# Token rows in a recommender kernel: every second gather adds its rows in the DMA, additions with a lag of three groups

## The chip, the cores and the metric

The kernel runs on one core of one Trainium2 chip. The metric is the device time of one launch in microseconds (us), as the median of several runs without a profile. The kernel before takes 5566.13 us (three runs, 5557.75 to 5580.29).

## What is computed

A batch of 16,384 samples goes through embedding lookups and a small MLP. The reference, cut to what matters:

```
tok = word_emb[token_idx].mean(axis=1)      # 32 rows of 300 floats from a table of 50,000
e1  = emb_mh1[mh1_idx].mean(axis=1)         # 20 rows of 64, likewise e2 and e3
o1  = emb_oh1[oh1_idx]                      # one row of 64, likewise o2 to o4
emb = concatenate([tok, e1, e2, e3, o1, o2, o3, o4], axis=1)      # 748 wide
wide = sums of one-column tables at the same indices
h = relu(emb @ W1 + b1); h = relu(h @ W2 + b2); h = relu(h @ W3 + b3)
return sigmoid(h @ Wd + bd + wide)
```

Only the first line is touched by the change: for each sample the sum of 32 rows of `word_emb`.

## The kernel before

The samples are cut into 128 tiles of 128, one sample on each partition, and four tiles make a block of 512. The main loop goes over the tiles, and inside a tile over `STEPS` = 11 steps. A step does a slice of three tiles' work, so that the engines overlap:

- `one_hots` (line 260): two VectorE (DVE) comparisons make one-hot rows for six pairs of samples of the current tile, one step ahead. Their inputs lie in SBUF.
- `counts` (line 278): 64-row matmuls on TensorE (PE) turn them into counts by table row. ScalarE (ACT) copies the counts from PSUM to FP8 (line 285).
- `tokens` (lines 180 to 206): the gathers of the token rows and their additions, of the current tile.
- `small_sums` (line 303): matmuls of the previous tile's counts with the small tables. DVE reduces the results into the tile `g` (line 310).
- `mlp` (`layer`, line 353): the MLP of the last complete block in float32 matmuls. ACT applies bias and ReLU (line 362).

The class `Paced` hands out the last three, as generators, in equal parts over the steps. Nothing reorders the instructions afterwards (`manual_schedule`): each engine executes its own in the order in which the loop writes them. When a block's four `g` tiles are complete, `transposed` (lines 345 and 346) turns them with PE and DVE into the MLP's input `x`. After the last tile there is one more iteration with only sums and MLP steps, and after it the last block's MLP runs alone.

The tokens: a tile of 128 samples needs 32 indirect DMAs, one for each index column. Each is issued by GpSimd (POOL) on line 188 and brings 128 rows of 300 floats, one to a partition. Four of them fill one buffer of the pool `tok`, which has three. A buffer's rows have a pitch of 320 floats and begin 32 floats into it. Three additions on DVE follow in program order, directly after a group's gathers: two rows with two rows (line 196, 600 elements), then one with one (line 204, 300 elements), then the sum into `g` (line 205); for a tile's first group the last two are one addition straight into `g` (line 202). There are eight groups a tile. The first gather of a group waits until DVE is done with the group three back, since that one held the same buffer. Every gather has one of eight DMA semaphores in turn, and waits for the gather eight back, which used it before.

Of the kernel before, what the change touches and what calls it, by code (L numbers as in the profile page):

```python
# [8 lines left out]
F32 = mybir.dt.float32  # L9
# [3 lines left out]
U32 = mybir.dt.uint32  # L13
AF = mybir.ActivationFunctionType
ALU = mybir.AluOpType
AX = mybir.AxisListType

P = 128
N_TOK, TOK_D = 32, 300
N_MH, EMB = 20, 64  # L20
ROW = EMB + 1
D1, D2, D3 = 1024, 512, 256
TOK_GROUP = 4
TOK_PITCH = 320
BLOCK = 512
HALF = P // 2
N_SMALL = 3 * N_MH + 4
# [1 line left out]
STEPS = -(-HALF // ONEHOT)  # L29
# [15 lines left out]
def kernel(  # L45
# [21 lines left out]
    nc = tc.nc  # L67
# [7 lines left out]
    for f in SMALL:  # L75
        n = -(-tables[f].shape[0] // P)
# [1 line left out]
        n_h += n  # L78
    PER_BANK = 512 // n_h

    tokp = ctx.enter_context(tc.tile_pool(name="tok", bufs=3))
    const = ctx.enter_context(tc.tile_pool(name="const", bufs=1))
    idxp = ctx.enter_context(tc.tile_pool(name="idx", bufs=2))
    keyp = ctx.enter_context(tc.tile_pool(name="keys", bufs=1))
# [40 lines left out]
    first = const.tile([P, 2, N_SMALL], I32, name="first")  # L125
# [10 lines left out]
    for part0 in range(0, n_h, PART):  # L136
        raw = cp.tile([P, PART, ROW], F32, name="raw", tag="counts")
        for f in SMALL:
            table, (h0, h1) = tables[f], slices[f]
            full, rest = divmod(table.shape[0], P)  # L140
            a, b = max(h0, part0), min(h0 + full, part0 + PART)
            if a < b:
                nc.sync.dma_start(
                    out=raw[:, a - part0 : b - part0, :],
                    in_=table[(a - h0) * P : (b - h0) * P, :].rearrange("(h p) d -> p h d", p=P),
# [4 lines left out]
        for a in range(0, PART, 23):  # L150
            b = min(a + 23, PART)
# [25 lines left out]
    bd_sb = const.tile([1, 1], F32, name="bd_sb")  # L177
    nc.scalar.dma_start(out=bd_sb, in_=bd)

    def tokens(g, it):  # L180

        for q in range(N_TOK // TOK_GROUP):

            space = tokp.tile([P, TOK_GROUP * TOK_PITCH + 64], F32, name="tok_rows")
            rows = space[:, 32 : 32 + TOK_GROUP * TOK_PITCH].rearrange("p (t d) -> p t d", d=TOK_PITCH)
            for t in range(TOK_GROUP):
                j = q * TOK_GROUP + t
                nc.gpsimd.indirect_dma_start(  # L188
                    out=rows[:, t, 0:TOK_D],
                    out_offset=None,  # L190
                    in_=word,
                    in_offset=bass.IndirectOffsetOnAxis(ap=it[:, j : j + 1], axis=0),
                )
            n = TOK_GROUP // 2
            while n > 1:
                nc.vector.tensor_add(  # L196
                    rows[:, 0:n, 0:TOK_D], rows[:, 0:n, 0:TOK_D], rows[:, n : 2 * n, 0:TOK_D]
                )
                n //= 2
            first, second = rows[:, 0, 0:TOK_D], rows[:, 1, 0:TOK_D]  # L200
            if q == 0:
                nc.vector.tensor_add(g[:, 0:TOK_D], first, second)
            else:
                nc.vector.tensor_add(first, first, second)  # L204
                nc.vector.tensor_add(g[:, 0:TOK_D], g[:, 0:TOK_D], first)  # L205
            yield 1

    def load_indices(blk):

# [202 lines left out]
    it, ix = load_indices(0)  # L412
# [3 lines left out]
    for t in range(tiles + 1):  # L416
        s = t % NSUB
        sums = None
        if before:
            sums = Paced(small_sums(*before), n_h + LULL, STEPS)  # L420
        if t < tiles:
            if s == 0 and t:
                it, sc = next_it, next_sc
            g = gp.tile([P, G_COLS], F32, name="g")
            cnt = cp.tile([P, 2, HALF, n_h], FP8, name="cnt", tag="counts")
            toks = Paced(tokens(g, it[:, s, :].bitcast(U32)), N_TOK // TOK_GROUP, STEPS)
        for i in range(STEPS):
# [12 lines left out]
            if sums:  # L440
                sums.go()
            if layers:
                layers.go()
        if before:
            sums.finish()
            gs.append(before[0])
            wides.append(wide_term(before[0]))
        before = (g, cnt) if t < tiles else None
        if len(gs) == NSUB:
            if layers:  # L450
                layers.finish()
            layers = Paced(mlp(t // NSUB - 1, transposed(gs), wides), mlp_size, NSUB * STEPS)
            gs, wides = [], []
# [40 lines left out]
```

## Time and profile before

| | us |
|---|---|
| median of three runs without a profile | 5566.13 |
| the profiled execution | 7340.1 |
| its span, first to last instruction | 7338.3 |
| POOL busy (4096 gathers of 0.997 us) | 4082.8 |
| PE busy, by the profile | 5808.1 |
| DVE busy | 3542.7 |
| ACT busy | 2657.3 |

The profiled execution is a third longer than the runs without a profile. An engine's busy time is the sum of its instructions' durations; ends of matmuls are modelled, so PE's is rough. In a group's line, `out<-in` are the program's tile names, followed by the number of instructions, their busy time in us, the mean ns of one, and the idle time of the engine just before them with what ended most of it. In a timeline each row has a start in us, a duration in us, the engine, the line, the operation, and in brackets the idle time before it with its releaser; `issue` means that the engine waited for nothing that the profile shows. The DMA queue `q0` is the one that POOL's gathers use; its share is that of 16 DMA engines over the span.

### The profile page before, as it was taken

How to read it: one execution, taken by the hardware profiler on the slowest of the kernel's cores; microseconds unless marked ns; L12 is line 12 of the kernel's file. 1: busy time of each engine (PE TensorE's matmuls, PEld its weight loads, DVE VectorE, ACT ScalarE, POOL GpSimd, SP SyncE). 2: the span in 40 equal slices, each digit the busy share in tenths (PEclk: the TensorE clock that was granted, in tenths of full speed). 3: DMA queues.
4: the chain of work that ended last, by engine and by line, in shares of the span. 5: the costliest groups of instructions: out<-in, count | busy, mean ns of one | idle time of the engine just before them, and what ended most of it. 6: DMA issues, size and time to landing. Idle time of an engine off the chain costs nothing.

```text
span 7338.3 us, 100239 instructions
## 1 busy us (share of the span) xinstructions
PE 5808.1 (79%) x40960; PEld 3442.6 (47%) x40960; DVE 3542.7 (48%) x6977; ACT 2657.3 (36%) x3383; POOL 4082.8 (56%) x4103
## 2 busy tenths in 40 slices
PE   2688888888778787888878788878877878888789
PEld 2444444444444444444444444444444444444444
DVE  4444445445444454445445445445544444445442
ACT  4333333333333333333333333333333333333332
POOL 5555555555555555555555555555555555555551
PEclk8798888888888888888899998888898989888899
DMA  4333333333333333333333333333333333333330
GB/s 130 94 89 92 88 89 90 91 90 88 88 90 89 88 85 90 89 88 90 93 89 94 90 90 89 91 86 91 88 89 90 88 87 90 93 89 88 86 91 25
DMA packets 242809, 652.34 MB, mean 89 GB/s; under 512 B 105631, under 2 KB 109471, under 8 KB 242347
## 3 DMA queue, kind: packets, MB, share of 16 engines
q0 software_dynamic: 196608, 629.41, 31.9%
q1 hardware_dynamic: 42738, 10.83, 0.8%
q8 instruction: 320, 5.24, 0.3%
q10 hardware_dynamic: 3001, 5.69, 0.2%
q14 instruction: 142, 1.16, 0.1%
HBM read 645.59 MB, written 0.07 MB: 88 GB/s over the span
## 4 chain that ended last, share of the span: by engine, by line
PE 59%; another core or an unknown queue 20%; ACT 10%; issue 7%; DVE 3%; DMA 0%; SPq 0%; DVEq 0%; ACTq 0%
PE ph L353 27%; PE pg L303 21%; PE pc L278 9%; ACT cnt L285 9%; PE pt L345 1%; ACT h L362 1%; DVE x L346 1%; DVE g L310 1%; PE po L375 1%; PE pk L243 0%; PE po L377 0%; DMA raw<-in_mh_dram 0%; DVE slice L260 0%; DVE tok_rows L196 0%
## 5 line engine op out<-in xcount | busy, mean ns | idle before, releaser
L188 POOL DMA_INDIRECT tok_rows<-in_word_emb_dram,it x4096 | 4081.9, 997 | 3120.9 <-DVE g L205 1202.3
L285 ACT ACTIVATE cnt<-pc 128x828 fp8e3<-128x828 f32 (+1 forms) x2816 | 2239.5, 840 | 3521.0 <-remote 1890.0
L303 PE MATMUL pg<-terms,cnt 128*128 128x195 bf16 x17664 | 2142.2, 271 | 372.5 <-issue 308.3
L260 DVE TENSOR_TENSOR row<-iota,sc 128x768 bf16<-128x768 bf16 (+1 forms) x1408 | 765.2, 543 | 2667.3 <-remote 1545.4
L303 PEld LDWEIGHTS <-cnt 128*128 128x128 fp8e3 x17664 | 1748.2, 147 | 629.6 <-issue 485.2
L353 PE MATMUL ph<-x,w_sb 128*128 128x512 f32 (+1 forms) x3072 | 1600.2, 647 | 27.1 <-issue 26.1
L278 PE MATMUL pc<-slice,row 64*128 64x138 bf16 x16384 | 858.3, 231 | 940.4 <-ACT cnt L285 640.7
L278 PEld LDWEIGHTS <-row 64*128 64x128 bf16 x16384 | 558.1, 97 | 2050.2 <-issue 1556.8
L353 PE MATMUL ph<-h,w_sb 128*128 128x512 f32 x2560 | 1341.1, 648 | 26.5 <-issue 24.6
L353 PEld LDWEIGHTS ph<-x,w_sb 128*128 128x128 f32 (+1 forms) x3072 | 579.6, 209 | 502.4 <-issue 489.1
L260 DVE TENSOR_TENSOR slice<-iota,sc 128x828 bf16<-128x828 bf16 (+1 forms) x1408 | 808.7, 574 | 0.0
L196 DVE TENSOR_TENSOR tok_rows<-tok_rows 128x600 f32<-128x600 f32 x1024 | 795.2, 777 | 1.0 <-DMA tok_rows<-in_word_emb_dram,it 0.7
L353 PEld LDWEIGHTS ph<-h,w_sb 128*128 128x128 f32 x2560 | 485.3, 210 | 415.5 <-issue 415.4
L362 ACT ACTIVATE h<-ph,b_sb 128x512 f32<-128x512 f32 x448 | 308.3, 688 | 948.6 <-PE ph L353 495.9
L310 DVE TENSOR_REDUCE g<-pg 128x130 f32<-128x390 f32 (+1 forms) x512 | 251.6, 510 | 787.3 <-remote 286.4
L204 DVE TENSOR_TENSOR tok_rows<-tok_rows 128x300 f32<-128x300 f32 x896 | 423.7, 473 | 30.8
L205 DVE TENSOR_TENSOR g<-g,tok_rows 128x300 f32<-128x300 f32 x896 | 422.0, 471 | 30.7
L346 DVE TENSOR_SCALAR x<-pt,scale 128x512 f32<-128x512 f32 (+1 forms) x192 | 139.6, 749 | 116.1 <-PE pt L345 74.9
L345 PE MATMUL pt<-ident,g 128*128 128x128 f32 (+1 forms) x768 | 132.3, 311 | 71.3 <-DVE x L346 70.3
L345 PEld LDWEIGHTS pt<-ident,g 128*128 128x128 f32 (+1 forms) x768 | 92.6, 154 | 110.0 <-DVE x L346 100.5
L243 PE MATMUL pk<-ident_bf,keys 128*128 128x128 bf16 x128 | 23.7, 241 | 86.7 <-DVE keys L238 85.0
L285 ACT ACT_TABLE_LOAD x31 | 39.8, 1283 | 143.2 <-PE pc L278 143.2
(35 smaller groups left out, 458.7 us busy)
## 6 DMA issues: line engine op xcount, KB each, us to landing
tok_rows<-in_word_emb_dram,it POOLq DMA_INDIRECT x4096
ix<-in_idx_dram SPq DMA_DIRECT2D x128, 32.0 KB
w_sb<-in_W_dram ACTq DMA_DIRECT2D x6, 512.0 KB
w_sb<-in_W_dram ACTq DMA_DIRECT2D x1, 2048.0 KB
it<-in_idx_dram SPq DMA_DIRECT2D x32, 64.0 KB
out_dram<-h SPq DMA_DIRECT2D x32, 2.0 KB
raw<-in_mh_dram SPq DMA_DIRECT2D x1, 422.5 KB
w_sb<-in_W_dram ACTq DMA_DIRECT2D x1, 256.0 KB
```

The costliest lines, as they stand in the source:

```text
L188: nc.gpsimd.indirect_dma_start(out=rows[:, t, 0:TOK_D], out_offset=None, in_=word, in_offset=bass.IndirectOffsetOnAxis(ap=it[:, j : j + 1] ...
L196: nc.vector.tensor_add(rows[:, 0:n, 0:TOK_D], rows[:, 0:n, 0:TOK_D], rows[:, n : 2 * n, 0:TOK_D])
L204: nc.vector.tensor_add(first, first, second)
L205: nc.vector.tensor_add(g[:, 0:TOK_D], g[:, 0:TOK_D], first)
L260: nc.vector.tensor_tensor(one[:, 0:rows, :].rearrange("p i (n d) -> p i n d", d=2), iota[:, 0:n].rearrange("p (n d) -> p n d", d=2).unsque ...
L278: nc.tensor.matmul(pc[:, f, k * n_h : (k + 1) * n_h], hot[0][half, k0 + k, :], hot[1][half, k0 + k, :], start=True, stop=True,)
L285: nc.scalar.activation(cnt[:, :, b + k0 : b + k0 + n, :].rearrange("l f k h -> l f (k h)"), pc[:, :, 0 : n * n_h], AF.Copy, scale=0.5, sat ...
L303: nc.tensor.matmul(pg[:, j, :], by_slice[:, :, h], terms[:, h, :], start=(h == h0), stop=(h == h1 - 1))
L310: nc.vector.tensor_reduce(g[:, at : at + n * ROW].rearrange("p (f d) -> p f d", f=n), pg[:, 0:n, :].rearrange("p f (c d) -> p f d c", c=3) ...
L345: nc.tensor.transpose(pt[:kk, s * P : (s + 1) * P], chunk(g, k), ident)
L353: nc.tensor.matmul(ph, weights[:kk, k, m * P : (m + 1) * P], src[:kk, k, :], start=(k == 0), stop=(k == len(kks) - 1),)
L362: nc.scalar.activation(dst[:, m, :], ph, AF.Relu, bias=bias[:, m : m + 1])
```

## The change

A group now has two row buffers, side by side without padding, and stands for four gathers: two plain ones that fill it, and two that add their rows to it in the DMA (`compute_op` add). Plain and adding gathers alternate: between the plain gathers of a group stand the adding gathers of the group before it. The order on POOL is: plain for group q, part 0; add for group q-1, part 0; plain for q, part 1; add for q-1, part 1. This runs on over the borders of tiles. An adding gather waits until the plain gather of the same part, five places before it on POOL, has landed. DVE's additions for a group come three groups later: the two halves into one (300 elements), and the sum into `g` (300 elements); for a tile's first group it is one addition into `g`. The pool `tok` has six buffers in place of three. So the last groups of a tile are added up during the next tile's first steps; `last_tokens` does what is left after the last tile, ahead of the final iteration's steps. The number of gathers stays 4096. Instructions on PE and ACT and their order are as before.

```diff
-TOK_GROUP = 4
-TOK_PITCH = 320
+TOK_GROUP = 2
+TOK_LAG = 3
...
-    tokp = ctx.enter_context(tc.tile_pool(name="tok", bufs=3))
+    tokp = ctx.enter_context(tc.tile_pool(name="tok", bufs=2 * TOK_LAG))
...
+    under_way = []
+
+    def gather(rows, t, it, j, op):
+        nc.gpsimd.indirect_dma_start(
+            out=rows[:, t * TOK_D : (t + 1) * TOK_D],
+            out_offset=None,
+            in_=word,
+            in_offset=bass.IndirectOffsetOnAxis(ap=it[:, j : j + 1], axis=0),
+            compute_op=op,
+        )
+
+    def add_up(rows, g, first):
+        a, b, n = rows[:, 0:TOK_D], rows[:, TOK_D : 2 * TOK_D], TOK_D
+        if first:
+            nc.vector.tensor_add(g[:, 0:n], a, b)
+        else:
+            nc.vector.tensor_add(a, a, b)
+            nc.vector.tensor_add(g[:, 0:n], g[:, 0:n], a)
+
     def tokens(g, it):
...
+        for q in range(N_TOK // (2 * TOK_GROUP)):
+            rows = tokp.tile([P, TOK_GROUP * TOK_D], F32, name="tok_rows")
             for t in range(TOK_GROUP):
...
+                gather(rows, t, it, q * 2 * TOK_GROUP + t, ALU.bypass)
+                if under_way:
+                    old, _, old_it, old_q = under_way[-1]
+                    gather(old, t, old_it, (old_q * 2 + 1) * TOK_GROUP + t, ALU.add)
+            under_way.append((rows, g, it, q))
+            if len(under_way) > TOK_LAG:
+                rows, to, _, old_q = under_way.pop(0)
+                add_up(rows, to, old_q == 0)
             yield 1
+
+    def last_tokens():
+        rows, _, it, q = under_way[-1]
+        for t in range(TOK_GROUP):
+            gather(rows, t, it, (q * 2 + 1) * TOK_GROUP + t, ALU.add)
+        for rows, g, _, q in under_way:
+            add_up(rows, g, q == 0)
...
-            toks = Paced(tokens(g, it[:, s, :].bitcast(U32)), N_TOK // TOK_GROUP, STEPS)
+            toks = Paced(tokens(g, it[:, s, :].bitcast(U32)), N_TOK // (2 * TOK_GROUP), STEPS)
+        else:
+            last_tokens()
```

More of the change, by code (lines that the diff above doesn't have):

```diff
@@ L180, in tokens @@
     def tokens(g, it):
-        for q in range(N_TOK // TOK_GROUP):
-            space = tokp.tile([P, TOK_GROUP * TOK_PITCH + 64], F32, name="tok_rows")
-            rows = space[:, 32 : 32 + TOK_GROUP * TOK_PITCH].rearrange("p (t d) -> p t d", d=TOK_PITCH)
+        for q in range(N_TOK // (2 * TOK_GROUP)):
+            rows = tokp.tile([P, TOK_GROUP * TOK_D], F32, name="tok_rows")
             for t in range(TOK_GROUP):
[L187 to L205, printed above, removed]
-            yield 1
```

## The prediction

> **What bounds the kernel now.** I read the page's busy shares first, then the costliest groups, then the waits of POOL, then the timeline of POOL and of PE.
>
> ```profile
> span 7338.3 us, 100239 instructions
> ...
> PE 5808.1 (79%) x40960; PEld 3442.6 (47%) x40960; DVE 3542.7 (48%) x6977; ACT 2657.3 (36%) x3383; POOL 4082.8 (56%) x4103
> ...
> q0 software_dynamic: 196608, 629.41, 31.9%
> ...
> L188 POOL DMA_INDIRECT tok_rows<-in_word_emb_dram,it x4096 | 4081.9, 997 | 3120.9 <-DVE g L205 1202.3
> ```
>
> By shares PE looks like the bound. But this profiled execution took 7340.1 us (span 7338.3) and the median without a profile is 5566.13, so PE's 5808 us of busy time cannot all be real: it is longer than the whole unprofiled run. The span holds stretches in which every engine stands still, and the unprofiled run has no room for them. So I ask what each engine needs when nothing holds it up.
>
> POOL first. Its timeline, in a stretch where it has buffers:
>
> ```profile
> 3003.55 0.95 POOL L188 DMA_INDIRECT tok_rows<-in_word_emb_dram,it  x1 [0.30 <-issue]
> 3004.81 0.95 POOL L188 DMA_INDIRECT tok_rows<-in_word_emb_dram,it  x1 [0.30 <-issue]
> 3012.30 0.94 POOL L188 DMA_INDIRECT tok_rows<-in_word_emb_dram,it  x1 [6.54 <-DVE g L205]
> ```
>
> A gather (128 rows of 300 floats) keeps POOL 0.95 us, and the next starts 0.30 us after it: 1.25 us from start to start. The mean is 0.997 us, so 4096 gathers need 4096 x (0.997 + 0.305) = 5333 us. The first starts at 38 us and the last ends at 7204, 134 us before the end (last additions, last sums, last MLP). 38 + 5333 + 134 = 5505 us: 61 us, 1.1%, under the unprofiled median. In the profile POOL idles besides (us in total, times, longest):
>
> ```profile
> POOL tok_rows L188 <- DVE g L205: 1202.3, 337, 10.0
> ...
> POOL tok_rows L188 <- DVE g L202: 753.6, 110, 16.4
> ```
>
> The 1956 us behind DVE are waits for a free row buffer, in steps that PE held up; they are the slack of the profiled execution (7338 - 5505 = 1833 us), and without the profile 61 us of it are left. POOL is the bound, at about 99%.
>
> PE next. In a dense stretch, one step of the main loop to the next:
>
> ```profile
> 7197.05 0.54 PE L278 MATMUL pc<-slice,row 64*128 64x138 bf16 x12
> ...
> 7200.54 0.54 PE L278 MATMUL pc<-slice,row 64*128 64x138 bf16 x12
> ```
>
> 3.49 us a step, 11 steps a tile are 38.4 us, and about 2 us of a tile are its share of a block's transposes and last layer (3022.1 to 3029.9 in the timeline, over four tiles): 40.4 us, against 32 x 1.302 = 41.7 us on POOL. PE is second by about 1.3 us a tile, 170 us in all. DVE needs 3542.7 / 128 = 27.7 us a tile and ACT 20.8.
>
> Last, DVE's additions, and what they do to POOL:
>
> ```profile
> L196 DVE TENSOR_TENSOR tok_rows<-tok_rows 128x600 f32<-128x600 f32 x1024 | 795.2, 777 | 1.0 <-DMA tok_rows<-in_word_emb_dram,it 0.7
> ...
> L204 DVE TENSOR_TENSOR tok_rows<-tok_rows 128x300 f32<-128x300 f32 x896 | 423.7, 473 | 30.8
> L205 DVE TENSOR_TENSOR g<-g,tok_rows 128x300 f32<-128x300 f32 x896 | 422.0, 471 | 30.7
> ```
>
> The timeline shows a gather beside them:
>
> ```profile
> 3015.78 0.78 DVE L196 TENSOR_TENSOR tok_rows<-tok_rows 128x600 f32<-128x600 f32 x1
> 3016.05 1.33 POOL L188 DMA_INDIRECT tok_rows<-in_word_emb_dram,it  x1 [0.30 <-issue]
> ...
> 3016.59 0.47 DVE L204 TENSOR_TENSOR tok_rows<-tok_rows 128x300 f32<-128x300 f32 x1
> ```
>
> DVE hardly waits for rows (1.0 us). A gather beside such additions takes 1.33 us instead of 0.95. Over all gathers the excess is 997 - 949 (the median) = 48 ns, 195 us.
>
> **What the Trainium skill says.** "SBUF — State Buffer", Who interferes with whom: a Vector instruction with two SBUF inputs contends with a GpSimd instruction that reads SBUF. The trace agrees that gathers beside such additions are longer (1.33 against 0.95 us). "DMA: Bandwidth & Descriptors", SWDGE vs HWDGE vs iDMA: accumulating DMAs go by GpSimd alone, and an operation is one read and one write descriptor; "GPSIMD Engine Reference", When to use GPSIMD: one core of a pair writes the read descriptors, the other the write descriptors. The trace agrees as far as it shows POOL busy for each gather. "Collectives: The Full Stack", The bandwidth ceiling: an add in the DMA engine needs two source reads, so two read descriptors a chunk, and its measured rate was about half a copy's. No run here shows that yet; the step that decides rests on it.
>
> **The change, part by part.** *Additions on DVE.* Removed: 1024 x 0.777 + 896 x (0.473 + 0.471) + 128 x 0.470 = 1701 us. Added: 15 a tile of 300 elements, 1920 x 0.471 = 904 us. 797 us less on DVE, all of it beside POOL's work, so worth nothing directly. Indirectly it shortens gathers. If the 195 us belong to all two-input operations by time (1701 us of additions, 1574 us of one-hots on line 260), 24% goes, 47 us; if to the additions alone, 47%, 92 us. Without the profile the same operations stand closer by 7338/5566 = 1.32: 62 to 121 us. I take 80 us gained.
>
> *Waits for buffers.* A plain gather waits for the additions of the group six buffers back, which stand three steps back in DVE's order; an addition needs gathers that POOL began two steps back. Before, POOL could be from 0 to 3 groups ahead, with 8 gathers between the two demands; now there are 16. That can give back at most the 61 us left; PE's floor stands 170 us lower. I count 0, as some of the 61 is PE's own jitter; bounds 0 to 61 gained.
>
> *Number of gathers.* Unchanged, 4096, and so the 0.305 us between them.
>
> *Accumulating gathers.* 2048 of them; the trace shows none. Below: nothing, if the write descriptor alone carries the add (I exclude a gain: the same rows are addressed). Above: if the read side has twice the descriptors and is what takes the 0.949 us, another 0.949. A part of 0.949 is start-up that isn't repeated, and the second address needs no index. I take 0.38 us, an estimate: 40% of the row. 2048 x 0.38 = 778 us on POOL, which is the bound, so on the path. Both ends: 0 and 1944 us.
>
> *The new wait.* Each accumulating gather waits until its plain one, five gathers earlier, has landed; behind it on POOL's queue stand all later gathers, and who needs those is DVE three groups on, with one-hots and so PE and ACT behind. From the DMA records a gather lands about 1.6 us after POOL is done with it, 2.5 us after its start; five starts are 6.5 us. 4 us of cover: cost 0. A landing later than that would be paid on POOL in full.
>
> *DMA engines.* 31.9% of 16 engines in 7338 us is 0.57 us a gather and engine. If an accumulating one takes twice that, the mean is 0.86 against a pitch of about 1.5: hidden. It becomes the bound only at 2 x 1.5 - 0.57 = 2.4 us, 4.3 times a plain one.
>
> *Start and end.* The last two accumulating gathers (about 2 x 1.6 us) start before the tail's sums, which need PE first; 3 us at most, within its 134 us of cover. The padding of the row buffers goes; no row prices it, and I take 0, within the DMA margin above.
>
> Sum: 5505 - 80 + 778 = 6203 on the profile's terms, plus the 61 us by which the median stands above: **6264, I say 6260 us**. The profiled execution itself has 1833 us of slack on POOL, so its span should grow much less, to 7300 to 7700.
>
> **The rivals.** *R1, the other side: the accumulate is free on POOL.* Then 5566 - 80 = 5486 us, and 5425 with all of the 61 us of waits gone too. For it: no second descriptor may be needed where the engine reads its own destination; against it, the skill's two reads. It is decided by POOL's extra per accumulating gather: under 80/2048 = 39 ns the kernel gets faster, over that slower. *R2: nothing measurable.* Extra of 25 to 53 ns: 5538 to 5594. *R3: the DMA engines become the bound.* If rows of an accumulate go one by one and it takes 2.9 us an engine (five times), the mean is 1.73, 4096 x 1.73 + 172 = 7260 us. For it: rows now travel four to a packet; against it: 68% of the engines' time is idle.
>
> **How the numbers follow.** 0.5% of 5566 (5538 to 5594) is about what a measurement can tell from no change. Chances: slower by POOL's generation 0.56, R1 0.25, R2 0.08, R3 0.11; so faster 0.25, same 0.08, slower 0.67. The main case's own range, with an extra of 0.10 to 0.74 us, is 5690 to 7000. For 8 in 10 I reach down to R1's end, 5425, and leave most of R3 and the upper end of the doubling out: 5425 to 7000.
>
> **What would show it.** In the changed kernel's profile the gathers should fall into two kinds: one at 0.95 us, one near 1.33. Should all be 0.95, the main step is wrong and R1 holds. Under R3, gathers stay short and POOL waits for the landing of tok_rows, with q0's share over 60%. DVE's busy time should be near 2745 us. Were PE the real bound now, even 0.38 us would cost only what exceeds 170 us.

## The result and the profile after

The changed kernel takes 6826.92 us (median of four runs, 6822.81 to 6833.73), beside 5566.45 us for the kernel before (four runs, 5557.75 to 5580.29): a ratio of 1.2263, 95% interval 1.2235 to 1.229. It is 1260 us slower; the forecast was 694 us slower. The profiled execution took 6833.73 us, so here the profile and the unprofiled runs agree. They don't for the kernel before, whose profiled execution took 7340.1 us; on two of the three chips of the experiments below its median is 7662 and 7674 us, on the third 5552 us. So each experiment stands beside the kernel before on its own chip.

From the page of the changed kernel, in its order: span, busy shares of the engines, POOL in 40 slices of the span, the gathers' DMA queue, the chain that ended last, and the groups of the gathers and of DVE's additions.

```profile
span 6831.9 us, 99374 instructions
...
PE 5522.3 (81%) x40960; PEld 3323.5 (49%) x40960; DVE 2737.4 (40%) x5953; ACT 2632.1 (39%) x3383; POOL 5435.6 (80%) x4103
...
POOL 6888888888888888888888888888888888888882
...
q0 software_dynamic: 393216, 629.41, 53.4%
...
POOL 48%; issue 22%; DMA 21%; PE 4%; DVE 4%; POOLq 0%; ACT 0%; DVEq 0%; SPq 0%; ACTq 0%
...
L183 POOL DMA_INDIRECT tok_rows<-in_word_emb_dram,it x4096 | 5434.8, 1327 | 1285.5 <-issue 1088.1
...
L196 DVE TENSOR_TENSOR tok_rows<-tok_rows 128x300 f32<-128x300 f32 x896 | 421.8, 471 | 3232.8 <-DMA tok_rows<-in_word_emb_dram,it 3232.8
```

The mean gather went from 0.997 to 1.327 us. POOL's idle time fell from 3120.9 to 1285.5 us, and of that 37.3 stand before the first gather and 1248.2 are the 4095 steps from one gather to the next, the longest of them 0.317 us. So POOL is never held up: busy 5434.8, idle 1285.5, and 111.6 us that are left, nearly all of them after the last gather, are the whole span, 6831.9. The chain's 21% for the DMA are no wait of POOL: 460 of its 0.3 us steps are put down to a landing, and there the chain goes through the transfer, beside which POOL worked on. DVE, which waited 1.0 us for rows before, now waits 3232.8 us for them: the other engines follow POOL.

The timeline of POOL in the changed kernel (start, duration, and in brackets the idle time before it and what ended it):

```profile
3018.84 1.55 POOL L183 DMA_INDIRECT tok_rows<-in_word_emb_dram,it  x1 [0.30 <-issue]
3020.69 0.99 POOL L183 DMA_INDIRECT tok_rows<-in_word_emb_dram,it  x1 [0.30 <-issue]
3021.99 1.54 POOL L183 DMA_INDIRECT tok_rows<-in_word_emb_dram,it  x1 [0.30 <-issue]
3023.83 0.99 POOL L183 DMA_INDIRECT tok_rows<-in_word_emb_dram,it  x1 [0.30 <-issue]
```

There are two kinds. Over all gathers with no two-input DVE operation beside them, an adding one takes 1.546 us on average and a plain one 0.990 us. In the kernel before such a gather took 0.948 (0.945 in a profile of it at full pace, further down). And the waits of the changed kernel (us in total, times, longest):

```profile
DVE tok_rows L196 <- DMA tok_rows<-in_word_emb_dram,it: 3232.8, 806, 5.3
...
POOL tok_rows L183 <- issue: 1088.1, 3570, 0.3
```

No gather waits longer than the usual 0.3 us. So neither the landing of the plain gathers nor a free buffer costs POOL anything, and q0's 53.4% leaves the DMA engines room.

### The profile page after: what moved, and what is told of

The parts are those of the page before. It is cut to its first block, busy times and chain, and to the rows that moved or that the text cites. A ratio compares the mean times of both kernels' runs of the same rounds, so it can differ in the third digit from the quotient of the medians.

```text
span 6831.9 us, 99374 instructions
## 1 busy us (share of the span) xinstructions
PE 5522.3 (81%) x40960; PEld 3323.5 (49%) x40960; DVE 2737.4 (40%) x5953; ACT 2632.1 (39%) x3383; POOL 5435.6 (80%) x4103
## 3 DMA queue, kind: packets, MB, share of 16 engines
q0 software_dynamic: 393216, 629.41, 53.4%
## 4 chain that ended last, share of the span: by engine, by line
POOL 48%; issue 22%; DMA 21%; PE 4%; DVE 4%; POOLq 0%; ACT 0%; DVEq 0%; SPq 0%; ACTq 0%
POOL tok_rows L183 48%; DMA tok_rows<-in_word_emb_dram,it 21%; PE ph L367 1%; PE po L389 1%; DVE x L360 1%; PE pt L359 1%; DVE g L324 1%; DVE tok_rows L196 0%; PE po L391 0%; DVE g L197 0%; PE pg L317 0%; DMA raw<-in_mh_dram 0%; DVE slice L274 0%; DVE row L274 0%; POOLq L183 0%
## 5 line engine op out<-in xcount | busy, mean ns | idle before, releaser
L183 POOL DMA_INDIRECT tok_rows<-in_word_emb_dram,it x4096 | 5434.8, 1327 | 1285.5 <-issue 1088.1
L299 ACT ACTIVATE cnt<-pc 128x828 fp8e3<-128x828 f32 (+1 forms) x2816 | 2207.8, 838 | 3174.8 <-PE pc L292 3172.0
L317 PE MATMUL pg<-terms,cnt 128*128 128x195 bf16 x17664 | 1962.5, 264 | 563.1 <-DVE g L324 563.1
L317 PEld LDWEIGHTS <-cnt 128*128 128x128 fp8e3 x17664 | 1683.8, 146 | 731.6 <-issue 585.0
L196 DVE TENSOR_TENSOR tok_rows<-tok_rows 128x300 f32<-128x300 f32 x896 | 421.8, 471 | 3232.8 <-DMA tok_rows<-in_word_emb_dram,it 3232.8
L367 PE MATMUL ph<-x,w_sb 128*128 128x512 f32 (+1 forms) x3072 | 1573.1, 640 | 0.0
L292 PEld LDWEIGHTS <-row 64*128 64x128 bf16 x16384 | 524.4, 98 | 1728.4 <-DVE slice L274 1100.3
L292 PE MATMUL pc<-slice,row 64*128 64x138 bf16 x16384 | 793.7, 231 | 650.9 <-DVE slice L274 630.6
L367 PE MATMUL ph<-h,w_sb 128*128 128x512 f32 x2560 | 1314.3, 640 | 0.0
L194 DVE TENSOR_TENSOR g<-tok_rows 128x300 f32<-128x300 f32 x128 | 60.3, 471 | 426.8 <-DMA tok_rows<-in_word_emb_dram,it 426.8
L389 PE MATMUL po<-h,wd_sb 128*1 128x512 f32 x128 | 97.4, 906 | 0.0
```

The lines of the kernel that those rows point to most:

```text
L183: nc.gpsimd.indirect_dma_start(out=rows[:, t * TOK_D : (t + 1) * TOK_D], out_offset=None, in_=word, in_offset=bass.IndirectOffsetOnAxis(ap ...
L196: nc.vector.tensor_add(a, a, b)
L292: nc.tensor.matmul(pc[:, f, k * n_h : (k + 1) * n_h], hot[0][half, k0 + k, :], hot[1][half, k0 + k, :], start=True, stop=True,)
L299: nc.scalar.activation(cnt[:, :, b + k0 : b + k0 + n, :].rearrange("l f k h -> l f (k h)"), pc[:, :, 0 : n * n_h], AF.Copy, scale=0.5, sat ...
L317: nc.tensor.matmul(pg[:, j, :], by_slice[:, :, h], terms[:, h, :], start=(h == h0), stop=(h == h1 - 1))
L367: nc.tensor.matmul(ph, weights[:kk, k, m * P : (m + 1) * P], src[:kk, k, :], start=(k == 0), stop=(k == len(kks) - 1),)
```

## The experiments

The theory after the result: POOL is the bound in both kernels, and an adding gather costs POOL 0.60 us more than a plain one, as such. Against it stand: the new order and its waits (the time would stay without the add); the shape of the transfer, since an adding gather sends each row as a packet of its own, 393216 packets on q0 where 196608 were (any transfer that computes would cost the same); the bytes that an add moves, pressing back on POOL; the padding that the change took away; and DVE's additions beside the gathers. Eleven more kernels, and the changed kernel once more, tell these apart.

### The new schedule without the adds

All gathers become plain; everything else stays.

```diff
-                    gather(old, t, old_it, (old_q * 2 + 1) * TOK_GROUP + t, ALU.add)
+                    gather(old, t, old_it, (old_q * 2 + 1) * TOK_GROUP + t, ALU.bypass)
...
-            gather(rows, t, it, (q * 2 + 1) * TOK_GROUP + t, ALU.add)
+            gather(rows, t, it, (q * 2 + 1) * TOK_GROUP + t, ALU.bypass)
```

> The changed kernel with every adding gather made plain: it overwrites its rows, so half of the token rows are left out of the sum; buffers, order, waits and lag stay. Theory (the add itself costs POOL 0.60 us a gather): all gathers near 0.95 us, and 4096 x (0.95 + 0.305 + 0.06 of DVE contention) + 150 = 5540 us, near 5480 if the longer slack gives the leftover waits back. Rival (the new order, its waits or the row buffers without padding cost it): stays above 6200 us.

Measured: 7609.61 us, where the kernel before takes 7662.13 on the same chip: ratio 0.9923 (0.9898 to 0.9947). Taken by the number alone, the time lies on the rival's side, above 6200 us; but both expectations were made for a chip on which the kernel before takes 5566 us, so the gathers have to decide. Its gathers in the page, and its longest-lasting waits:

```profile
L183 POOL DMA_INDIRECT tok_rows<-in_word_emb_dram,it x4096 | 4028.6, 984 | 3453.3 <-DVE g L197 1789.6
```

```profile
POOL tok_rows L183 <- DVE g L197: 1789.6, 317, 16.1
DVE row L274 <- remote: 1714.2, 260, 11.4
ACT cnt L299 <- remote: 1691.5, 401, 11.3
```

The mean gather is 0.984 us and POOL waits 1789.6 us for DVE: on this chip something other than POOL bounds the kernel (the last section comes back to it). What it shows all the same is that the schedule costs nothing against the kernel before on this chip, and that all gathers are short again (0.948 us alone) once the add is gone. The time of the schedule on a chip where POOL bounds the kernel comes from the 64-row kernel further down.

The changed kernel itself, on a second such chip:

> The changed kernel once more, beside the kernel before on the same chip. In the last four runs the kernel before stood at 7662 us and the variants without an add near it, while in the runs that the prediction was scored on it stood at 5566 us. Theory (the changed kernel is paced by POOL alone, so PE's standstills hide behind it): 6820 to 6835 us again, wherever it runs, and faster than the kernel before where that one stands at 7660. Rival (the standstills add to both): above 8000 us there.

Measured: 6846.69 us, beside 7674.38 for the kernel before: ratio 0.8913 (0.8884 to 0.8942). The changed kernel takes the same here as in the first comparison, within 0.3%, though 12 us more than the expected range; it is the kernel before that takes 2108 us more. On this chip the change is a gain, and only because of that. A POOL-paced kernel can be compared across chips here, the kernel before cannot. The lag of the additions alone, with plain groups of four, was not tried.

### Which part of the adding gather costs POOL

**One packet a row and a converting transfer, without the add.** The adding gathers become plain ones that cast to bf16 on the way, into the same places.

```diff
+        to = rows[:, t * TOK_D : (t + 1) * TOK_D]
...
-            out=rows[:, t * TOK_D : (t + 1) * TOK_D],
+            out=to if op else to.bitcast(BF16)[:, 0:TOK_D],
...
-            compute_op=op,
+            compute_op=ALU.bypass,
...
-                    gather(old, t, old_it, (old_q * 2 + 1) * TOK_GROUP + t, ALU.add)
+                    gather(old, t, old_it, (old_q * 2 + 1) * TOK_GROUP + t, None)
```

> The changed kernel with every adding gather replaced by a plain one that casts its rows to bf16 into the same place; the second half of the rows is left out of the sum as numbers. [...] If the 0.60 us come from a second read descriptor a row, the casting gathers take about 0.95 to 1.0 us and the kernel about 5560 us. If they come from one packet a row and the compute path as such, casting gathers take about 1.55 us and the kernel stays near 6820 us.

Measured: 7638.66 us, ratio 0.9963 (0.9947 to 0.9979) to the kernel before at 7662.13. From its page and its timeline of POOL:

```profile
q0 software_dynamic: 393216, 472.12, 34.4%
...
L184 POOL DMA_INDIRECT tok_rows<-in_word_emb_dram,it x4096 | 4029.4, 984 | 3450.5 <-DVE g L198 1786.0
```

```profile
3004.20 0.95 POOL L184 DMA_INDIRECT tok_rows<-in_word_emb_dram,it  x1 [0.30 <-issue]
3005.45 0.95 POOL L184 DMA_INDIRECT tok_rows<-in_word_emb_dram,it  x1 [0.30 <-issue]
```

The queue has the 393216 packets of the changed kernel, so each casting row travels alone; yet one of these two gathers casts and one doesn't, and both take 0.95 us (alone, 0.950 and 0.946 on average). The gathers came as expected; the expected time of 5560 us did not, for the reason given for the all-plain kernel. So neither one packet a row nor a cast costs POOL anything. What remains is the add itself, with the second source read that the prediction named; no run separates these two.

**Half the bytes.** The adding gathers bring half a row, 150 floats.

```diff
-            out=rows[:, t * TOK_D : (t + 1) * TOK_D],
+            out=rows[:, t * TOK_D : t * TOK_D + (TOK_D if op == ALU.bypass else TOK_D // 2)],
...
-            in_=word,
+            in_=word if op == ALU.bypass else word.rearrange("v (h d) -> (v h) d", h=2),
```

> The changed kernel with adding gathers of 150 floats a row in place of 300; half of each second row is left out, and other table rows are read. The descriptors stay as many, the bytes of adding gathers halve. Theory (POOL writes descriptors): adding gathers stay at 1.55 us, the kernel at 6800 to 6830 us. Rival (POOL is held up by busy DMA engines or by full descriptor rings): adding gathers fall towards 1.25 us and the kernel to about 6200 us.

Measured: 6771.12 us (two runs). From its page:

```profile
q0 software_dynamic: 393216, 472.12, 37.6%
...
L183 POOL DMA_INDIRECT tok_rows<-in_word_emb_dram,it x4096 | 5373.5, 1312 | 1285.2 <-issue 947.6
```

The queue's share fell from 53.4% to 37.6%. The adding gathers still take 1.547 us alone, with the same 0.3 us between gathers. So neither the bytes of an add nor the load that they put on the queue presses back on POOL. The 56 to 76 us that it is faster than the changed kernel, and below the expected range by 29, are 15 ns a gather. They lie in the excess over a gather that has no two-input DVE operation beside it, which is 44 ns on average here and 59 in the changed kernel (more on it further down).

**Half the rows.** The adding gathers take 64 partitions.

```diff
-            out=rows[:, t * TOK_D : (t + 1) * TOK_D],
+            out=rows[0 : P if op == ALU.bypass else HALF, t * TOK_D : (t + 1) * TOK_D],
...
-            in_offset=bass.IndirectOffsetOnAxis(ap=it[:, j : j + 1], axis=0),
+            in_offset=bass.IndirectOffsetOnAxis(ap=it[0 : P if op == ALU.bypass else HALF, j : j + 1], axis=0),
```

> The changed kernel with adding gathers on 64 partitions in place of 128; the other 64 samples' second rows are left out. Half the descriptors. If 1.55 us is start-up s plus a price for each row: with s = 0.5, as the first-order guess, adding gathers take 1.0 us and the kernel about 5700 us; were all of the extra a fixed price for the mode, 1.3 us and about 6300 us.

Measured: 6523.63 us (two runs). Its POOL timeline:

```profile
3005.61 1.42 POOL L183 DMA_INDIRECT tok_rows<-in_word_emb_dram,it  x1 [0.30 <-issue]
3007.33 1.00 POOL L183 DMA_INDIRECT tok_rows<-in_word_emb_dram,it  x1 [0.30 <-DMA tok_rows<-in_word_emb_dram,it]
```

An adding gather of 64 rows takes 1.416 us alone, 0.131 less than one of 128. If the price of rows is a straight line through these two points, it is 2.04 ns a row, and 1.546 - 2 x 0.131 = 1.28 us are not set by the rows. Both expected values, 1.0 and 1.3 us, were too low, and so were both expected times.

**The same for plain gathers**, in the new schedule and on a chip where the kernel before takes 5552.36: the 64-row gathers are plain.

```diff
-                    gather(old, t, old_it, (old_q * 2 + 1) * TOK_GROUP + t, ALU.add)
+                    gather(old, t, old_it, (old_q * 2 + 1) * TOK_GROUP + t, ALU.bypass, HALF)
...
-            gather(rows, t, it, (q * 2 + 1) * TOK_GROUP + t, ALU.add)
+            gather(rows, t, it, (q * 2 + 1) * TOK_GROUP + t, ALU.bypass, HALF)
```

> The changed kernel with every adding gather replaced by a plain one on 64 partitions (half of the second rows overwritten, the others left out). For the price of a row in plain gathers: with 64 rows fewer in adding gathers their median fell from 1.548 to 1.417 us, 2.0 ns a row. If an adding row costs twice a plain one, plain gathers of 64 rows take 0.949 - 0.065 = 0.88 us; if the extra 0.60 us is mostly a fixed price of the mode, the plain row costs about as much as the adding one and they take 0.82 us.

Measured: 5494.67 us (one run). From its page, and three of its gathers in the timeline:

```profile
span 5492.9 us, 100398 instructions
...
PE 5153.3 (94%) x40960; PEld 3129.1 (57%) x40960; DVE 2750.0 (50%) x5953; ACT 2629.8 (48%) x3383; POOL 4090.7 (74%) x4103
...
L183 POOL DMA_INDIRECT tok_rows<-in_word_emb_dram,it x4096 | 4089.8, 998 | 1288.0 <-issue 1177.2
```

```profile
3009.43 0.96 POOL L183 DMA_INDIRECT tok_rows<-in_word_emb_dram,it  x1 [0.31 <-issue]
3010.69 0.96 POOL L183 DMA_INDIRECT tok_rows<-in_word_emb_dram,it  x1 [0.30 <-issue]
3011.96 0.90 POOL L183 DMA_INDIRECT tok_rows<-in_word_emb_dram,it  x1 [0.30 <-issue]
```

A plain gather takes 0.958 us with 128 rows and 0.903 with 64, more than either expectation. By the same straight line that is 0.86 ns a row (about 0.7 against the 0.949 of the kernel before), and about 0.85 us that the rows don't set. So of the 0.60 us that the add costs, an estimated (2.04 - 0.8) x 128 = 0.16 us are by the row, and about 0.43 are a fixed price of the adding DMA. And the new schedule itself costs little where POOL bounds it: with 0.055 us more for each of its 2048 short gathers this kernel would take an estimated 5494.67 + 113 = 5607 us, 1% more than the kernel before. That answers the rival of the new order and its waits.

### Does the price add up

Adds in every second group only.

```diff
-                    gather(old, t, old_it, (old_q * 2 + 1) * TOK_GROUP + t, ALU.add)
+                    gather(old, t, old_it, (old_q * 2 + 1) * TOK_GROUP + t, ALU.add if old_q % 2 else ALU.bypass)
...
-            gather(rows, t, it, (q * 2 + 1) * TOK_GROUP + t, ALU.add)
+            gather(rows, t, it, (q * 2 + 1) * TOK_GROUP + t, ALU.add if q % 2 else ALU.bypass)
```

> The changed kernel with every second group's adding gathers made plain (they overwrite, so a quarter of the token rows is left out of the sum). Theory (POOL's time is the sum of its gathers, 0.60 us more for each of 1024 adding ones): POOL needs 4096 x (0.95 + 0.305 + 0.06) + 1024 x 0.60 + 160 = 6160 us. If PE's standstills come only when PE is driven densely, they are absent or hidden at this pace too and the kernel takes 6150 to 6250 us; if they come at this pace already, it ends above 6600 us, POOL waiting for buffers.

Measured: 6100.68 us, ratio 1.0989 (1.097 to 1.1007) on the chip where the kernel before takes 5552.36. From its page:

```profile
span 6098.9 us, 99374 instructions
...
L183 POOL DMA_INDIRECT tok_rows<-in_word_emb_dram,it x4096 | 4700.2, 1148 | 1285.3 <-issue 1037.6
```

POOL's sum is again the whole span: 4700.2 + 1285.3 leaves 113.4 us, where the changed kernel has 111.6. The time is 49 us under the expected range: the expectation counted 60 ns of excess a gather, and the trace has 37. 1024 adds more (this kernel to the changed one) cost 6826.9 - 6100.7 = 726 us, 0.71 us each. Gathers with no two-input operation beside them give 0.63 of it, and the rest is the excess, 37 ns a gather here and 59 in the changed kernel. Against the kernel before, 548 us for the first 1024 adds are 0.54 each, the new schedule included. So POOL pays for either half of the adds; the size differs by what lies beside the gathers.

### The padding

The changed kernel with the old pitch of 320 floats and 32 floats ahead:

```diff
+TOK_PITCH = 320
...
-            out=rows[:, t * TOK_D : (t + 1) * TOK_D],
+            out=rows[:, t * TOK_PITCH : t * TOK_PITCH + TOK_D],
...
-        a, b, n = rows[:, 0:TOK_D], rows[:, TOK_D : 2 * TOK_D], TOK_D
+        a, b, n = rows[:, 0:TOK_D], rows[:, TOK_PITCH : TOK_PITCH + TOK_D], TOK_D
...
-            rows = tokp.tile([P, TOK_GROUP * TOK_D], F32, name="tok_rows")
+            rows = tokp.tile([P, TOK_GROUP * TOK_PITCH + 64], F32, name="tok_rows")[:, 32 : 32 + TOK_GROUP * TOK_PITCH]
```

> The changed kernel with the row buffers padded as in the kernel before (pitch of 320 floats, 32 floats ahead). If the missing padding made plain gathers 0.99 us in place of 0.95, they fall back and the kernel gains about 80 us (6760); if it is the adding gathers around them, nothing moves: 6830 to 6850 us.

Measured: 6850.91 us, ratio 1.2338 (1.2318 to 1.2359). That is within 0.4% of the changed kernel on its two other chips; plain gathers take 0.990 us as without padding. The padding plays no part.

### The order on POOL, and DVE's additions beside the gathers

**Two plain, then two adding.** One more loop line lets the two plain gathers go ahead of the two adding ones.

```diff
                 gather(rows, t, it, q * 2 * TOK_GROUP + t, ALU.bypass)
+            for t in range(TOK_GROUP):
                 if under_way:
```

> The changed kernel with a group's two plain gathers first and then the two adding ones of the group before, in place of alternating. The plain gathers of the changed kernel take 0.99 us where nothing of DVE is beside them, 0.95 in the kernel before. If a plain gather is longer because it follows an adding one, one plain gather in two is back at 0.95 and the kernel gains about 40 us; if it is longer because of the adding DMAs under way in the engines, both stay at 0.99. The kernel stays at 6780 to 6840 us.

Measured: 6717.58 us (two runs), 1.9% under the changed kernel's 6846.69 on the same chip. Four gathers of its timeline:

```profile
3006.86 1.00 POOL L183 DMA_INDIRECT tok_rows<-in_word_emb_dram,it  x1 [0.30 <-DVE keys L253]
3008.16 0.97 POOL L183 DMA_INDIRECT tok_rows<-in_word_emb_dram,it  x1 [0.30 <-issue]
3009.44 1.57 POOL L183 DMA_INDIRECT tok_rows<-in_word_emb_dram,it  x1 [0.30 <-issue]
3011.31 1.55 POOL L183 DMA_INDIRECT tok_rows<-in_word_emb_dram,it  x1 [0.30 <-DMA tok_rows<-in_word_emb_dram,it]
```

That is 62 us below the expected range, and neither of its two cases came. With no two-input operation beside it, the first plain gather after an add has a median of 1.001 us, the second 0.972, the adding ones 1.565 and 1.553. So a plain gather is somewhat longer near adds, the more so directly behind one; but these medians together (1.273 us a gather) are no lower than the changed kernel's (1.268). The gain lies in the excess over them: the mean gather is 1.299, so the excess is 26 ns, where the changed kernel has 59, and 62 in its run on this chip. By the traces that is 148 us; 18 of them go back into the longer medians, which leaves 130, the whole gain of 129. DVE's operations delay gathers less in this order (the tables further down). This version is the fastest found that computes everything with adds in the DMA; its 6718 us are still more than the 5552 to 5566 us that the kernel before takes where POOL bounds it.

**The kernel before without its additions**:

```diff
-            n = TOK_GROUP // 2
-            while n > 1:
-                nc.vector.tensor_add(
-                    rows[:, 0:n, 0:TOK_D], rows[:, 0:n, 0:TOK_D], rows[:, n : 2 * n, 0:TOK_D]
-                )
-                n //= 2
...
+            nc.vector.tensor_reduce(g[:, 0:1], rows[:, :, 0:2], AX.XY, ALU.add)
```

> The kernel before with DVE's additions of token rows left out (a reduction over two elements of each row takes their place in the order, so that buffers are released as before); the token sums are left out. If the additions carry most of the 48 ns a gather by which 997 exceeds 949, the mean gather falls to 955 to 965 ns; if one-hots carry them by their share of the time, to 974 ns. The time follows POOL (5566 to about 5420 us) where PE doesn't stand still, and doesn't move where it does.

Measured: 7548.15 us (two runs), ratio 0.9824 (0.9781 to 0.9867) beside 7674.38. Its gathers:

```profile
L188 POOL DMA_INDIRECT tok_rows<-in_word_emb_dram,it x4096 | 3975.5, 971 | 3442.0 <-DVE g L196 2264.2
```

Without any additions the mean gather falls from 997 to 971 ns: 26 of the 48 ns of excess go with them, and 22 stay with the one-hots. So the additions carry about half of it at this pace, which is their share of the time, as the second case had it (974 ns expected), and not most of it.

**The kernel before with one reduction for three additions**, a one-input operation over three new rows and the sum so far:

```diff
...
+            parts = rows[:, 0 : 4 if q else 2, 0:TOK_D].rearrange("p t d -> p d t")
+            nc.vector.tensor_reduce(to, parts, AX.X, ALU.add)
+            rows = following
...
```

> The kernel before with the three additions of a group replaced by one reduction over three new rows and the sum so far, which has one SBUF input; eleven groups of three gathers (the first of two) in place of eight of four; the whole computation. If additions with two SBUF inputs are what prolongs gathers, the mean gather falls from 997 to about 960 ns and the kernel gains up to 150 us where POOL is the bound (about 5420 us against 5566). Rival: the strided reads make the reduction slow (over 2 us) and DVE becomes late: slower by several per cent.

Measured: 7418.61 us, ratio 0.9665 (0.9631 to 0.9698) beside 7674.38. From its page:

```profile
L202 DVE TENSOR_REDUCE tok_rows<-tok_rows 128x300 f32<-128x1200 f32 (+1 forms) x1280 | 2697.6, 2107 | 22.3 <-DMA tok_rows<-in_word_emb_dram,it 20.1
...
L189 POOL DMA_INDIRECT tok_rows<-in_word_emb_dram,it x4096 | 4096.3, 1000 | 3179.1 <-DVE tok_rows L202 1648.1
```

The expectation was that an operation with one input leaves POOL alone and that gathers become shorter. The mean gather is 1.000 us, no shorter than 0.997: a miss. The timeline shows that the reductions are not the reason:

```profile
2987.86 2.23 DVE L202 TENSOR_REDUCE tok_rows<-tok_rows 128x300 f32<-128x1200 f32 x1
2988.57 0.95 POOL L189 DMA_INDIRECT tok_rows<-in_word_emb_dram,it  x1 [0.30 <-issue]
```

The gather lies wholly beside the reduction and takes 0.95 us. Over the whole trace, 1114 gathers beside a reduction of token rows and no two-input operation take 0.948 us on average; 1104 beside both such a reduction and a two-input operation take 1.134, and these 1104 x 0.186 = 205 us are nearly the whole excess of 4096 x 0.052 = 213. So reductions don't delay gathers, as the Trainium skill has it ("SBUF — State Buffer", Who interferes with whom: a reduction never contends with GpSimd on trn2), but the one-hots then delay them more than before (in the kernel without additions theirs were 92 us). A reduction takes 2.1 us for three new rows where the three additions took 0.777 + 0.473 + 0.471 = 1.72 for four, so DVE has more to do. The kernel is 3.4% faster on a chip where POOL isn't the bound; why was not settled, and what it does where the kernel before takes 5552 was not tried.

### The kernel before at full pace

The wish was to see whether the data has to do with the chips on which the kernel before takes 7670 us, by setting the tables' terms and all weights to zero in SBUF:

```diff
+    for zeroed in (terms, w1_sb, w2_sb, w3_sb, wd_sb):
+        nc.vector.memset(zeroed, 0.0)
```

> The kernel before with the MLP's weights and the small tables set to zero on the chip ahead of the loop (the MLP and the small sums are left out as numbers; instructions and order stay). If PE's standstills come from the power that its multiplications draw, they go or shrink and the kernel falls from about 7670 to between 5570 and 6500 us. If they come from the number of instructions in a time, or from how they are recorded, it stays at 7600 to 7700 us.

Measured: 5583.12 us, ratio 1.0054 (1.0037 to 1.007), on the chip where the kernel before takes 5552.36. For its question it says nothing, since there was nothing to take away on that chip. But its profile is that of the order of before at full pace (31 us, 0.5%, over the kernel before on this chip; what these are is not known):

```profile
span 5587.7 us, 100245 instructions
...
PE 5160.1 (92%) x40960; PEld 3130.5 (56%) x40960; DVE 3569.8 (64%) x6982; ACT 2631.6 (47%) x3383; POOL 4121.0 (74%) x4103
...
L191 POOL DMA_INDIRECT tok_rows<-in_word_emb_dram,it x4096 | 4120.1, 1006 | 1339.4 <-issue 1099.5
```

POOL's idle time is 1339.4 us here against the 1285.5 of the changed kernel: 54 us of waits in all. So POOL was the bound, as the prediction read from a profile that hid it: (5587.7 - 54) / 5587.7 is 99%. The gathers take 0.945 us alone and 1.006 on average, an excess of 60 ns.

## Why the prediction was right and wrong

The side was right, and so was the mechanism; the loss was nearly twice the forecast. With the zero-weight kernel as the kernel before at full pace (span 5587.7) and the profile of the changed one (6831.9), both taken apart in POOL's terms, the difference of 1244.2 us is this:

| term of the sum | forecast, us | measured, us | from |
|---|---|---|---|
| accumulating gathers | +778 | +1231 | 2048 x (1.546 - 0.945) |
| plain gathers | 0 | +92 | 2048 x (0.990 - 0.945) |
| less DVE work beside the gathers | -80 | -7 | excess of 58.8 against 60.5 ns |
| waits for buffers | 0 | -54 | POOL's idle time, 1285.5 - 1339.4 |
| after the last gather | 0 | -17 | 111.6 - 128.2 |
| sum | +698 | +1245 | |

*What bounds the kernel.* Right. POOL fills the changed kernel's span without a gap, as it fills 99% of the zero-weight kernel's.

*Accumulating gathers.* This is the step that failed, in its size: "I take 0.38 us, an estimate: 40% of the row." Measured are 0.60 us, 63%. The 40% rested on no line of the profile; the text had an upper and a lower bound and an argument between them, that a part of the 0.949 is start-up that isn't repeated. That is half right: the rows do cost little. A plain gather is about 0.85 us of fixed time and 0.1 us of rows; but the adding one has a fixed time of 1.28, so the fixed part is what grew, by about 0.43, and the rows give 0.16 more. It lies inside the bounds that the text gave, 0 to 0.949. The price of 0.60 instead of 0.38 alone moves the forecast by 2048 x 0.22 = 451 us, most of the 567 us by which it fell short. Why the fixed part grows isn't shown. The second source read of an add in the DMA, on which the prediction leaned (the Trainium skill, "Collectives: The Full Stack", The bandwidth ceiling), fits with what was found in one respect: a cast, which has one source, is free, and an add is not. But no run looks inside POOL, and twice the read descriptors would let one expect a price by the row, which is only 0.16 of the 0.60.

*Plain gathers.* The forecast left them at 0.95 without a word on it. They take 0.990 in the changed kernel, and 1.001 where they directly follow an add in the blocked order, while a plain gather behind a casting or a 64-row plain one has 0.946 and 0.958. So something of an add stays with the gathers behind it; half the rows (1.00) or padding (0.990) make no difference. The kernel with half the adds shows it fade: five plain gathers follow each second add there, and with no two-input operation beside them they take 0.986, 0.969, 0.952, 0.945 and 0.946 us on average. What it is that stays is open.

*Less DVE work.* This term was mis-sized too, 80 us where 7 were measured. DVE's busy time is 2737.4 us, as forecast (2745), and the gain still isn't there. Every gather of four traces, by the two-input DVE operations that it overlaps, with the excess over a gather that overlaps none (number of gathers: us in total):

| beside the gather | before, profiled at 7340 | zero weights | changed | blocked order |
|---|---|---|---|---|
| additions only | 540: 50.9 | 1144: 26.4 | 828: 0.8 | 680: 0.2 |
| one-hots and the like only | 908: 41.6 | 1463: 139.9 | 983: 154.0 | 745: 70.0 |
| both | 607: 104.5 | 777: 79.4 | 882: 85.6 | 1001: 36.0 |
| per gather, ns | 48 | 60 | 59 | 26 |

In the changed kernel gathers beside additions alone are hardly longer. But that gain was small at full pace (26.4 us), and the one-hots, which the change leaves as they are, take about as much as all of them took: they delay 983 gathers by 157 ns each where they lie alone. The forecast split the excess of a profile at 7340 us by time and scaled it by 1.32; the split between the two kinds of operation was another at full pace.

The kind of operation is not what decides, as the same traces show when the gathers are sorted by what DVE does at the moment at which a gather starts:

| at the gather's start | zero weights | changed | blocked order |
|---|---|---|---|
| no two-input operation is running, and one begins during the gather | 1315: 0.4 | 1055: 0.5 | 822: 0.7 |
| an addition is running | 811: 57.5 | 721: 76.1 | 896: 28.4 |
| a one-hot or the like is running | 1258: 189.8 | 917: 164.2 | 708: 78.5 |

Nearly all of the excess lies with gathers that start while a two-input operation is running. One that begins later doesn't delay the gather, and a running addition delays it as well as a running one-hot does (105 and 179 ns on average in the changed kernel). The skill's page ("SBUF — State Buffer", Who interferes with whom) makes no difference between the two either: both have two SBUF inputs. The delay follows what is left of the operation: in the changed kernel, where no other follows at once, under 100 ns left cost nothing, 200 to 300 ns cost 132 on average, and 400 to 500 ns cost 339. The gathers beside additions alone get off because 797 of the 828 had run for 0.7 us or more when the addition began; DVE waits there for a landing. Two gathers of the changed kernel, the first with an addition that begins during it, the second with a one-hot running at its start:

```profile
3025.13 1.55 POOL L183 DMA_INDIRECT tok_rows<-in_word_emb_dram,it  x1 [0.30 <-issue]
3026.05 0.47 DVE L194 TENSOR_TENSOR g<-tok_rows 128x300 f32<-128x300 f32 x1 [1.11 <-DMA tok_rows<-in_word_emb_dram,it]
...
3027.94 0.59 DVE L274 TENSOR_TENSOR slice<-iota,sc 128x828 bf16<-128x828 bf16 x1
3028.28 1.67 POOL L183 DMA_INDIRECT tok_rows<-in_word_emb_dram,it  x1 [0.30 <-issue]
```

So the forecast's measure, DVE's time, was the wrong one. Fewer gathers of the changed kernel start beside a two-input operation than in the zero-weight kernel (1638 against 2069), but each of them is delayed longer (147 ns against 119), and the two cancel. What in a gather's start is held up, no view shows.

*Waits.* The waits for buffers went away, within the 0 to 61 us that the text had set as its bounds. The new wait of an adding gather for its plain one costs nothing, as forecast: no gap on POOL is longer than the usual one. Its price was rightly set at 0: a plain gather lands 4.7 us before its adding one starts (median; 2.4 at the least), where the forecast had 4.

*DMA engines.* Right that they don't bound: 53.4% of q0, and POOL never waits for them. By q0's shares the mean is 0.534 x 6831.9 / 4096 = 0.89 us a gather and engine; forecast was 0.86. The third rival, at over 60%, falls. The first and second fall with the two kinds of gathers: the extra is 0.60 us, far above their 39 and 53 ns.

*The profiled execution* was forecast at 7300 to 7700 and took 6833.7. The forecast took the 1833 us of slack on POOL for a property of the profiler that a slower POOL would add to. They go with PE's standstills of the last section, which come without a profile too (7662 and 7674 us on two chips). In the changed kernel they are missing, or hidden behind POOL.

## What to carry to other kernels

Where POOL's issue of indirect DMAs bounds the kernel, price a change by POOL's time for each DMA, and not by the work that it saves on another engine: here 797 us less on DVE were worth about nothing (7 us), and each add in the DMA cost POOL 0.6 us on top of 0.95. Fewer bytes or rows hardly buy that back, since most of a gather's time on POOL doesn't depend on them. Where DVE's two-input operations lengthen gathers, count the gathers that start while one is running, and not DVE's time. And if a profiled execution is a third longer than the runs without a profile, work out each engine's time from its unhindered instructions, as here, and ask for the time of the kernel before on every chip on which something is compared with it.

## What was not expected of the hardware

**Casting is free for POOL where adding is not**: 0.950 us beside 0.946, though each row of 600 bytes travels as a packet of its own.

**A program of the same code takes 5552 us on one chip and 7670 on two others** (medians 7662 and 7674), every run of it, and the kernel before had both times in one comparison (profiled 7340.1, not profiled 5566). The lost time looks like this in the timeline of the profiled execution of before:

```profile
2921.99 0.54 PE L278 MATMUL pc<-slice,row 64*128 64x138 bf16 x12
...
2928.77 0.94 POOL L188 DMA_INDIRECT tok_rows<-in_word_emb_dram,it  x1 [0.30 <-issue]
2931.90 2.37 ACT L285 ACTIVATE cnt<-pc 128x828 fp8e3<-128x828 f32 x3 [11.11 <-remote]
2931.97 0.56 DVE L260 TENSOR_TENSOR row<-iota,sc 128x768 bf16<-128x768 bf16 x1 [8.90 <-remote]
...
2932.81 0.53 PE L278 MATMUL pc<-slice,row 64*128 64x138 bf16 x6 [4.86 <-ACT cnt L285]
```

PE's counts of 2921.99 are done after 0.54 us by the profile, but ACT and DVE, which need them, start only at 2931.9, after waits of 11.11 and 8.90 us that the profile can't trace to anything (`remote`); POOL runs on until its buffers are used up. ACT's waits of this kind come to 1890.0 us in that execution, and DVE's to 1545.4. The all-plain kernel has them too (1691.5 and 1714.2); the changed kernel and the zero-weight kernel show none. The changed kernel takes 6827 us in the first comparison and 6847 on the chip on which the kernel before takes 7674, and its padded version 6851 where the kernel before takes 5552. TensorE's mean granted clock is 0.88 to 0.89 in profiled executions with such waits (7340 to 7620 us), 0.98 in those of about 5500 to 5590, and 0.92 in the changed kernel; whether it is the cause or goes with it is open. The experiment meant for the cause ran where there was nothing to see.

**A strided reduction on DVE is slow**: 2.2 us to add up 4 x 300 floats on each partition, three new rows and the sum so far, beside 1.72 us for the three additions that add four new rows to the sum.
